# A graph layer on one core: four groups' last two tiles fetched row by row on SP's queue, with four smaller edits

## The chip, the cores and the metric

The kernel runs on one core of one Trainium2 chip. The metric is the device time of one execution in microseconds (us). Before the change the median of 3 runs is 2490.05 us (2479.22 to 2493.46).

## The reference

There are 12500 nodes with 64 features, and 200000 edges sorted by their destination, each with a source, a destination and 32 features of its own. Everything is float32.

```python
msg_in = concatenate([nodes[row], nodes[col], edge_features])      # 64 + 64 + 32
messages = relu(msg_in @ mW1 + mb1) @ mW2 + mb2                    # 160 -> 128 -> 64
aggregated = segment_sum(messages, col)
out = relu(concatenate([nodes, aggregated]) @ uW1 + ub1) @ uW2 + ub2
x = layernorm(x + out)
```

## The kernel before, in words

**Tables.** The first layer of the message network is linear, so it is split: A = x @ mW1[:64] and B = x @ mW1[64:128] + mb1 are computed once for all nodes (`products`, `chunk_a`, `chunk_b`) and stored in DRAM as tables of 128 numbers a row. An edge then needs a row of A (by source), a row of B (by destination) and its own features times mW1[128:].

**Tiles and groups.** 128 edges are a tile (1563 of them). Six tiles are a group s (261), two groups a supergroup g (131). The main loop runs over groups; each of the five engines has its instructions in one order, which is written by hand as the order of the calls in the loop. It is this order that decides what waits for what.

**One group.** SP loads windows of B (`windows`, L282 or L284: 32 consecutive rows of B serve one or several tiles, since edges are sorted by destination; the position comes from a register that L276 loads). SP also loads the destinations, broadcast over partitions, into the operand `l` (`loadd`, L233); DVE turns them into a one-hot selection by comparing with each partition's node number, which L243 prepares (`select`, L243, L245, L251); then SP loads the edge features into the other partitions of the same operand (`load`, L264), behind L245. PE multiplies `l` with the windows (`edge_part`, L374), which gives the B part and the edge part of all six tiles in PSUM (`pc`).

The A part comes in one of two ways. POOL gathers the rows of A of a tile by an indirect transfer, one for each tile (`gather`, L217), up to ten groups ahead into nine row buffers. Or, in 104 of the groups (the list `COPIED`, spaced by the rates in `PACE`), the last two tiles are not gathered: ACT and DVE copy the columns of x of the 2 x 128 source nodes out of a copy of x that lies in SBUF, one pair of columns in an instruction (`singly` on ACT, L345; `joined` on DVE, L352; their addresses are loaded into registers in L322), and PE multiplies them by the weights into `pc` (L377). These copies are spread over the iterations before the group that needs them.

`node_part` adds the gathered rows to `pc` on DVE and applies the relu on ACT (L401 and L402 for whole groups; L397, L398 and L399 for copied ones). `collect` sums h by destination with PE (L434), and counts edges (L431) for the bias term. Every eight groups or so a stretch of nodes is complete: `close` moves the sums and the counts from PSUM to SBUF (L448 and L449, both on ACT), `carry` takes the last 32 nodes over into the next stretch, and `update` to `store` compute and write the result (L471 to L525).

**How many windows.** One window serves 12 tiles at first and fewer as the loop goes on, since later edges lie sparser: 6 from group 32 on, 4 from 64, 3 from 98, 2 from 130, and one for every tile from group 196 on. SP's transfers for a group grow accordingly from one or less to six.

Of the kernel before, what the change touches and what calls it, by code (L numbers as in the profile page):

```python
# [24 lines left out]
SUB = 6  # L25
SUP = 12
NSUP = -(-NT // SUP)
NTP = NSUP * SUP
EPAD = NTP * P
NSUB = -(-NT // SUB)  # L30
WIN = 32
# [15 lines left out]
UW = UN + WIN  # L47
# [22 lines left out]
XBASE = 8320  # L70
U8 = mybir.dt.uint8
YBASE = XBASE + 4 * XCOLS
LEAD = 8
PACE = ((11, 0.413), (50, 0.44), (130, 0.424), (261, 0))
FINAL = 258


# [5 lines left out]
COPIED = []  # L83
for s in range(NSUB):
    while progress(s) >= len(COPIED) + 1 and s + 3 < FINAL:
        COPIED.append(s + 3)
LAST = 4 * (N - 1)
ACTS, CHUNK = 64, 8

# [14 lines left out]

UPD = updates()

UL = min(UB * P, -(-int(N * (1 - (UPD[-1] * SUB * P / E) ** 2) + WIN // 2) // 64) * 64)


@with_exitstack  # L110
def gnn_kernel(ctx: ExitStack, tc: tile.TileContext, x1T, x, eT, e_rows, src, src_row, dst, dst_row, wlist, wrow, wnext, whalf,
# [24 lines left out]
    nc = tc.nc  # L136
# [4 lines left out]
    A = dram.tile([NPAD, DH], F32, name="tab_a")  # L141
# [11 lines left out]
    col_a = const.tile([P, 2, P, 2], I32, name="col_a")  # L153
# [4 lines left out]
    xw = [const.tile([P, UB * P], F32, name=f"xw{k}") for k in range(2)]  # L158
# [17 lines left out]
    pidx = const.tile([P, 1], F32, name="pidx")  # L176
# [1 line left out]
    zero_b = const.tile([P, UW], BF, name="zero_b")  # L178

    cpool = ctx.enter_context(tc.tile_pool(name="cpsum", bufs=1, space=bass.MemoryType.PSUM))  # L180
    cps = cpool.tile([P, WIN + SUP], F32, name="cps")
    slot = cps[:, :WIN]
    drc = const.tile([P, NT], F32, name="drc")
    flag_i = const.tile([1, 1], I32, name="flag_i")
# [3 lines left out]
    wh = const.tile([P, NTP // 2], I32, name="wh")  # L188
# [11 lines left out]
    def tiles(s):  # L200
        return range(s * SUB, min((s + 1) * SUB, NT))

    def gathered_tiles(s):
        return tiles(s)[:SUB - 2 * (s in COPIED)]

    def gather(s):

# [14 lines left out]
    with tc.tile_pool(name="sup", bufs=2) as sup, tc.tile_pool(name="work", bufs=2) as work, tc.manual_schedule():  # L222
# [3 lines left out]
        def loadd(g):  # L226
# [6 lines left out]
                nc.sync.dma_start(l[q:q + WIN].bitcast(I32), dv[:, b].broadcast_to([WIN, SUP // 2, P]))  # L233
            L[g] = l

        def select(g, at=None):


            nt = min(SUP, NT - g * SUP)
            l = L[g]  # L240
            c = WIN + SUP // 2 * (g % 2)
            node = cps[:, c:c + SUP // 2]
            nc.vector.tensor_scalar(node, wh[:, g * SUP // 2:(g + 1) * SUP // 2], pidx, None, op0=ALU.add)  # L243
            for r in ([slice(0, P)] if g > 2 else [slice(q, q + WIN) for q in SK]):
                nc.vector.tensor_tensor(l[r], l[r].bitcast(I32),  # L245
                                        node[r].unsqueeze(2).broadcast_to([r.stop - r.start, SUP // 2, P]),
                                        op=ALU.is_equal)
            if at is not None:
                joined(at, 1, 3)
            s = sup.tile([P, SUP, WIN], F32, name="sel")  # L250
            nc.vector.tensor_tensor(s[:, :nt], slot.unsqueeze(1).broadcast_to([P, nt, WIN]),  # L251
                                    drc[:, g * SUP:g * SUP + nt].unsqueeze(2).broadcast_to([P, nt, WIN]),
                                    op=ALU.is_equal)
            S[g] = s
# [92 lines left out]
        def joined(s, part, of):  # L347

            todo = [(o, k, ACTS + e) for o, k, lo, hi in portion(s, P - ACTS) for e in range(lo, hi, 2)]
            for o, k, a, m in share(todo, part, of):  # L350
                for e, top, bot in addresses(k, a, m, ET.DVE):
                    nc.vector.tensor_tensor(o[:, e:e + 1].bitcast(I32), top.bitcast(I32), bot.bitcast(I32),  # L352
                                            op=ALU.bitwise_or)

        xc = {}

        def parts(n):

            if n == SUB:
                return [(slice(0, 2), SUB // 2)]  # L360
            return [(slice(b, b + 1), (n - b + 1) // 2) for b in range(2) if n > b]
# [18 lines left out]
        def node_part(s):  # L380

            n = len(tiles(s))
            pc = pcs.pop(s)
            h = work.tile([P, 2, SUB // 2, DH], F32, name="h")
            if s < XG:
                xt = xs.pop(s)
                for i in range(n):
                    k, b = divmod(i, 2)
                    q = 64 * b
                    nc.tensor.matmul(pc[:, b, k, :], xt[q:q + 64, k, :], w1a[q:q + 64], start=False,  # L390
                                     stop=i + 2 >= n)
                nc.scalar.activation(h, pc, AF.Relu)
            else:
                a = xg.pop(s)[0].rearrange("p (b k) f -> p b k f", b=2)
                if s in COPIED:
                    m = SUB // 2 - 1
                    nc.vector.tensor_tensor(h[:, :, :m], pc[:, :, :m], a[:, :, :m], op=ALU.add)  # L397
                    nc.scalar.activation(h[:, :, :m], h[:, :, :m], AF.Relu)  # L398
                    nc.scalar.activation(h[:, :, m:], pc[:, :, m:], AF.Relu)  # L399
                for b, m in parts(n) if s not in COPIED else []:  # L400
                    nc.vector.tensor_tensor(h[:, b, :m], pc[:, b, :m], a[:, b, :m], op=ALU.add)  # L401
                    nc.scalar.activation(h[:, b, :m], h[:, b, :m], AF.Relu)  # L402
            hs[s] = h
# [41 lines left out]
        def close(u):  # L445

            ps, pn = sums.pop(u)
            nc.scalar.copy(xw[u % 2][0:1, :UW], pn)  # L448
            nc.scalar.copy(sums_s[u % 2], ps)  # L449

        us = {}
# [117 lines left out]
        def zeros(i, n):  # L569

            w = XCOLS // n
            for t in (xtop[D:], xbot[:D]):
                nc.scalar.activation(t[:, i * w:(i + 1) * w], ident[:D, 0:1].broadcast_to([D, w]), AF.Copy, scale=0.0)
# [80 lines left out]
        for k, c in enumerate(range(0, NB, NCH)):  # L654
            chunk_a(c)
            if k == 0:
                chunk_b(0, [B0v, Bv])
            if k == 2:

                w0 = wint[:, :GE * SUP // SUB * LS]  # L660
                nc.vector.tensor_scalar(past, w0[:, GE * SUP // SUB * LS - 1:], float(EARLY - WIN), None, op0=ALU.is_gt)
                nc.vector.tensor_scalar(w0, w0, float(EARLY - WIN), None, op0=ALU.min)
                windows(0)
                windows(1)
            if k == 4:
                relative(0, 8 * SUP)
            if k == 6:
                offsets()
            if k == 9:
                select(0)  # L670
                load(0)
                counts(0)

        def rest(s):

            if 3 <= s < 9 and s % 2:
                others((s - 3) // 2 * 4, (s - 3) // 2 * 4 + 4)
            if 3 <= s < 11:
                zeros(s - 3, 8)
            if s == 9:  # L680
                columns_list()
            if s == 1:
                relative(8 * SUP, 8 * SUP + WCH)
            elif s == 2:
                relative(8 * SUP + WCH, NT)
                halves(4 * SUP, NTP // 2)
            elif s == BS:
                nc.sync.dma_start(wa, wrow.rearrange("o (p c) -> (o p) c", c=NSUP))
                nc.sync.dma_start(wb, wnext.rearrange("o (p c) -> (o p) c", c=NSUP))
# [12 lines left out]
            elif s == BS + 2:  # L702
                weights()
                checks()
# [49 lines left out]
        n = UPD[K - 1]  # L754
# [8 lines left out]
        for s in range(last + 2):  # L763
            g, j = divmod(s, SUP // SUB)
# [54 lines left out]
            if s == UPD[K - 1]:  # L819
                columns(K - 1)  # L820
            rest(s)
            joined(s, 2 if j == 0 and g + 1 < NSUP else 1, 3 if j == 0 and g + 1 < NSUP else 2)
            singly(s, 0, 1)
            if s in due and due[s] + 2 < K:
# [5 lines left out]
            if earlier(5) is not None:  # L830
# [4 lines left out]
                          skip_runtime_bounds_check_because="a count of edges")  # L835
    with tc.If(flag > 0), tc.tile_pool(name="gen", bufs=1) as up:
# [25 lines left out]
        first = up.tile([P, 1], F32, name="first")  # L862
        nc.vector.tensor_scalar(first, spare, -1.0, float(NPAD + P), op0=ALU.mult, op1=ALU.add)

        with tc.For_i(0, NT, 1) as t:
# [26 lines left out]
            pc = psum.tile([P, DH], F32, name="pcg", tag="pc")  # L892
# [4 lines left out]
            h = up.tile([P, DH], F32, name="hg")  # L897
# [104 lines left out]
```

## Time and profile before

| | us |
|---|---|
| median of 3 runs | 2490.05 |
| the profiled execution, in all | 2486.88 |
| its span, first to last instruction | 2485.1 |
| PE, ACT, POOL, DVE busy | 1630.3, 1612.1, 1280.4, 1118.3 |
| mean granted TensorE clock | 0.535 of full speed |

Busy time of an engine doesn't count the instructions of its sequencer: register loads, address arithmetic, semaphores and the issuing of transfers. SP does nothing else, so it has no busy share at all, and is read from the waits of its queue ("SPq") and from the timeline. "issue" is time in which an engine waited for nothing that the profile shows. In a row of waits stand the engine and the line, what was waited for, the time in all, how often, and the longest.

### The profile page before, as it was taken

The numbers are of one execution on the slowest core, as the hardware profiler recorded it, in microseconds if no ns is written. First come the engines' busy times: TensorE is split into PE (matmuls) and PEld (weight loads), VectorE is DVE, ScalarE is ACT, GpSimd is POOL, SyncE is SP. The second block draws the span as 40 slices with busy tenths as digits, with TensorE's granted clock in tenths as the row PEclk, the third lists the DMA queues.
The fourth block names the chain that finished last, engine by engine and source line by source line (L and its number), as shares of the span: only waits on it lengthen the run. The fifth ranks groups of instructions, "written<-read, shape, count | busy, mean of one in ns | idle before, by whom it ended". The sixth has DMA issues, their size and how long they took to land. (4 is left out here: it accounts for less than half of the span.)

```text
span 2485.1 us, 47640 instructions
## 1 busy us (share of the span) xinstructions
PE 1630.3 (66%) x9652; PEld 1392.7 (56%) x9652; DVE 1118.3 (45%) x7843; ACT 1612.1 (65%) x7232; POOL 1280.4 (52%) x1364
## 2 busy tenths in 40 slices
PE   1238575666566666666567666776667777777878
PEld 1237465655555555555555555555556656666666
DVE  0211554544444544445444444544544444544544
ACT  0015676767777767768776766776767776777754
POOL 7153455555555555545555555555555555555540
PEclk7565555555555555555555555555555555555556
DMA  5343232322222222222222222222222222222222
GB/s 131 104 120 84 71 91 78 89 78 71 69 67 65 74 64 72 68 68 72 71 71 75 76 69 74 78 75 76 74 75 73 75 78 79 76 77 74 80 72 53
DMA packets 207229, 191.63 MB, mean 77 GB/s; under 512 B 57243, under 2 KB 173297, under 8 KB 206945
## 3 DMA queue, kind: packets, MB, share of 16 engines
q0 software_dynamic: 43360, 86.92, 13.7%
q1 hardware_dynamic: 149040, 92.72, 13.5%
q10 hardware_dynamic: 14546, 8.93, 1.3%
q8 instruction: 91, 1.49, 0.3%
q14 instruction: 192, 1.57, 0.2%
HBM read 170.65 MB, written 17.76 MB: 76 GB/s over the span
## 5 line engine op out<-in xcount | busy, mean ns | idle before, releaser
L217 POOL DMA_INDIRECT xg<-tab_a,src_s x1295 | 1222.6, 944 | 1120.5 <-DVE h L401 403.3
L345 ACT ACTIVATE xc<-xtop,xbot 128x1 f32 x6656 | 1302.3, 281 | 296.7 <-issue 274.0
L352 DVE TENSOR_TENSOR xc<-xtop,xbot 128x1 int32 x6656 | 597.0, 154 | 630.8 <-issue 609.9
L434 PE MATMUL sums<-sel,h 128*128 128x32 f32 x3126 | 688.6, 385 | 140.0 <-issue 82.2
L434 PEld LDWEIGHTS sums<-sel,h 128*128 128x128 f32 x3126 | 655.9, 313 | 168.8 <-issue 82.7
L374 PE MATMUL pc<-rhs,l 64*128 64x128 f32 x3126 | 478.1, 436 | 355.3 <-DVE h L401 85.5
L374 PEld LDWEIGHTS pc<-rhs,l 64*128 64x128 f32 x3126 | 392.2, 309 | 431.7 <-issue 169.0
L245 DVE TENSOR_TENSOR l<-l,cps 128x768 f32<-128x768 int32 (+1 forms) x134 | 127.8, 954 | 167.9 <-remote 84.1
L402 ACT ACTIVATE h<-h 128x768 f32<-128x768 f32 (+1 forms) x148 | 122.5, 829 | 115.0 <-DVE h L401 100.1
L431 PEld LDWEIGHTS <-one 128*1 128x1 bf16 x1563 | 66.1, 83 | 225.0 <-issue 213.4
L431 PE MATMUL cnt<-sel,one 128*1 128x32 bf16 x1563 | 113.2, 188 | 112.8 <-issue 111.7
L401 DVE TENSOR_TENSOR h<-pc,xg 128x768 f32<-128x768 f32 (+1 forms) x148 | 140.4, 949 | 89.5 <-remote 30.4
L397 DVE TENSOR_TENSOR h<-pc,xg 128x512 f32<-128x512 f32 x104 | 71.8, 690 | 183.2 <-remote 71.6
L398 ACT ACTIVATE h<-h 128x512 f32<-128x512 f32 x104 | 64.8, 623 | 106.1 <-DVE h L397 83.4
L251 DVE TENSOR_TENSOR sel<-cps,drc 128x384 f32<-128x384 f32 x131 | 72.0, 549 | 102.0 <-PE sums L434 75.8
L377 PE MATMUL pc<-w1a,xc 64*128 64x128 f32 x416 | 82.9, 398 | 2.0 <-issue 2.0
L590 ACT COPY tb<-pb 128x512 f32<-128x512 f32 (+1 forms) x13 | 7.4, 569 | 114.6 <-remote 74.7
L580 PE MATMUL pb<-w1a,xtop 64*128 64x128 f32 x100 | 25.1, 435 | 84.8 <-DVE tb L588 59.5
L377 PEld LDWEIGHTS pc<-w1a,xc 64*128 64x128 f32 x416 | 73.8, 313 | 2.5 <-issue 2.5
L471 PE MATMUL pu<-xw,uz 128*128 128x448 f32 (+1 forms) x68 | 61.2, 1000 | 18.0 <-DVE h L401 12.4
L493 ACT COPY y<-py 128x256 f32<-128x256 f32 x33 | 12.0, 364 | 93.9 <-remote 67.8
L580 PEld LDWEIGHTS pb<-w1a,xtop 64*128 64x128 f32 x100 | 22.3, 325 | 87.2 <-DVE tb L588 61.3
(104 smaller groups left out, 965.7 us busy)
## 6 DMA issues: line engine op xcount, KB each, us to landing
l<-in_dst_row SPq DMA_DIRECT2D x262, 96.0 KB
l<-in_eT SPq DMA_DIRECT2D x262, 96.0 KB
xg<-tab_a,src_s POOLq DMA_INDIRECT x1295
rhs<-tab_b SPq DMA_DIRECT2D x361, 32.0 KB
tab_b<-tb SPq DMA_DIRECT2D x13, 512.0 KB
rhs<-tab_b SPq DMA_DIRECT2D x387, 16.0 KB
tab_a<-tb ACTq DMA_DIRECT2D x12, 512.0 KB
out<-y SPq DMA_DIRECT2D x33, 128.0 KB
```

What stands on the lines that cost most here:

```text
L217: nc.gpsimd.indirect_dma_start(out=a[:, i, :] if s < XG else a[:, i // 2, i % 2, :], out_offset=None, in_=A[:, :] if s >= XG else x[:, :], ...
L245: nc.vector.tensor_tensor(l[r], l[r].bitcast(I32), node[r].unsqueeze(2).broadcast_to([r.stop - r.start, SUP // 2, P]), op=ALU.is_equal)
L251: nc.vector.tensor_tensor(s[:, :nt], slot.unsqueeze(1).broadcast_to([P, nt, WIN]), drc[:, g * SUP:g * SUP + nt].unsqueeze(2).broadcast_to( ...
L345: nc.scalar.activation(o[:, e:e + 1], top.bitcast(F32), AF.Identity, bias=bot.bitcast(F32))
L352: nc.vector.tensor_tensor(o[:, e:e + 1].bitcast(I32), top.bitcast(I32), bot.bitcast(I32), op=ALU.bitwise_or)
L374: nc.tensor.matmul(pc[:, b, k, :], L[g][q:q + 64, m, :], rhs[g % 2][q:q + 64, w, :], start=s >= XG or k == 0, stop=s >= XG and not copied)
L377: nc.tensor.matmul(pc[:, b, k, :], xc[s][q:q + 64], w1a[q:q + 64], start=False, stop=True)
L397: nc.vector.tensor_tensor(h[:, :, :m], pc[:, :, :m], a[:, :, :m], op=ALU.add)
L401: nc.vector.tensor_tensor(h[:, b, :m], pc[:, b, :m], a[:, b, :m], op=ALU.add)
L402: nc.scalar.activation(h[:, b, :m], h[:, b, :m], AF.Relu)
L431: nc.tensor.matmul(pn[:, bass.ds(ws[i], WIN)], one, SB[g][:, k0 + i, :, 1], start=False, stop=ends and i == n - 1)
L434: nc.tensor.matmul(ps[:, bass.ds(ws[i], WIN)], h[:, i % 2, i // 2, :], S[g][:, k0 + i, :], start=False, stop=ends and i == n - 1)
```

## The change

Five things change.

1. Four further groups (the list `SINGLE`) are not gathered whole: as in the copied groups, POOL gathers four tiles of six. The rows of A of the other two tiles come by single transfers from table A, one for each edge: one partition, 512 bytes. SP issues them in `fetched`, called once an iteration near its end, for as many edges as `ROWPACE` allows (3.5 an iteration from group 12, 3.0 from 45, 2.3 from 90, 1.6 from 136, in even numbers), two transfers an edge; one register load brings the addresses of a portion. DVE adds the gathered part and the fetched part in two instructions.
2. `close` copies the counts on DVE, not on ACT.
3. The node numbers that L243 computed for each supergroup are computed in three long instructions (`first_nodes`) and kept in PSUM, 80 supergroups at a time.
4. In a copied group DVE adds into PSUM, in place, and ACT applies one relu to all six tiles.
5. `PACE` is raised by about 1.5%, so that 105 groups are copied.

```diff
-PACE = ((11, 0.413), (50, 0.44), (130, 0.424), (261, 0))
+PACE = ((11, 0.42), (50, 0.446), (130, 0.429), (261, 0))
...
+ROWPACE = ((12, 3.5), (45, 3.0), (90, 2.3), (136, 1.6))
+SINGLE, QUOTA = [], {}
+step, found = ROWPACE[0][0], 0.0
+while step < NSUB - 8:
+    done, a = 0, step
+    while done < P and step < NSUB - 8:
+        found += next(r for b, r in reversed(ROWPACE) if step >= b)
+        n = min(int(found) // 2 * 2, P - done)
+        found -= n
+        QUOTA[step] = len(SINGLE), done, done + n
+        done += n
+        step += 1
...
+    SINGLE.append(next(c for c in range(step + 1, NSUB) if c not in COPIED))
+    step = SINGLE[-1] + 1
...
+NODES = 80
...
-    cps = cpool.tile([P, WIN + SUP], F32, name="cps")
+    cps = cpool.tile([P, WIN + NODES * SUP // 2], F32, name="cps")
...
-        return tiles(s)[:SUB - 2 * (s in COPIED)]
+        return tiles(s)[:SUB - 2 * (s in COPIED or s in SINGLE)]
...
+        def first_nodes(a, b):
+            c = WIN + SUP // 2 * (a % NODES)
+            nc.vector.tensor_scalar(cps[:, c:c + SUP // 2 * (b - a)], wh[:, SUP // 2 * a:SUP // 2 * b], pidx, None, op0=ALU.add)
...
-            c = WIN + SUP // 2 * (g % 2)
+            c = WIN + SUP // 2 * (g % NODES)
             node = cps[:, c:c + SUP // 2]
-            nc.vector.tensor_scalar(node, wh[:, g * SUP // 2:(g + 1) * SUP // 2], pidx, None, op0=ALU.add)
...
+        def fetched(s):
+            if s not in QUOTA or QUOTA[s][1] == QUOTA[s][2]:
+                return
+            i, lo, hi = QUOTA[s]
+            k = SINGLE[i] - LEAD
+            if lo == 0:
+                xr[SINGLE[i]] = work.tile([P, 2, DH], F32, name="xr", bufs=1)
+            o = xr[SINGLE[i]]
+            _, v = nc.values_load_multi_w_load_instructions(
+                col_a[k % P:k % P + 1, k // P].rearrange("k e b -> k (e b)")[:, 2 * lo:2 * hi], engines=[ET.SP], min_val=XBASE,
+                max_val=YBASE + LAST, skip_runtime_bounds_check_because="sources are node numbers")
+            for e in range(lo, hi):
+                for b, first in enumerate((XBASE, YBASE)):
+                    w = v[2 * (e - lo) + b].with_bounds(min_val=first, max_val=first + LAST, guaranteed_mod_val=0, out_of_modulus=4)
+                    nc.sync.dma_start(o[e:e + 1, b], A4[bass.ds(w - first, 4), :].rearrange("c d -> (c d)").unsqueeze(0))
...
                 if s in COPIED:
                     m = SUB // 2 - 1
+                    nc.vector.tensor_tensor(pc[:, :, :m], pc[:, :, :m], a[:, :, :m], op=ALU.add)
+                    nc.scalar.activation(h, pc, AF.Relu)
+                if s in SINGLE:
+                    m = SUB // 2 - 1
                     nc.vector.tensor_tensor(h[:, :, :m], pc[:, :, :m], a[:, :, :m], op=ALU.add)
-                    nc.scalar.activation(h[:, :, :m], h[:, :, :m], AF.Relu)
-                    nc.scalar.activation(h[:, :, m:], pc[:, :, m:], AF.Relu)
+                    nc.vector.tensor_tensor(h[:, :, m], pc[:, :, m], xr[s], op=ALU.add)
+                    nc.scalar.activation(h, h, AF.Relu)
...
-            nc.scalar.copy(xw[u % 2][0:1, :UW], pn)
+            nc.vector.tensor_copy(xw[u % 2][0:1, :UW], pn)
...
+                first_nodes(0, 8)
                 select(0)
...
+            if s == 6:
+                first_nodes(8, NODES)
+            if s == 2 * NODES - 3:
+                first_nodes(NODES, NSUP)
...
             rest(s)
+            fetched(s)
             joined(s, 2 if j == 0 and g + 1 < NSUP else 1, 3 if j == 0 and g + 1 < NSUP else 2)
```

More of the change, by code (lines that the diff above doesn't have):

```diff
@@ L86 @@
         COPIED.append(s + 3)
+ROWPACE = ((12, 3.5), (45, 3.0), (90, 2.3), (136, 1.6))
[10 more added lines that the diff above has]
+        step += 1
+    if done < P:
+        QUOTA = {k: v for k, v in QUOTA.items() if k < a}
+        break
+    SINGLE.append(next(c for c in range(step + 1, NSUB) if c not in COPIED))
+    step = SINGLE[-1] + 1
 LAST = 4 * (N - 1)
@@ L355, in gnn_kernel @@
         xc = {}
+        A4 = A.rearrange("n (c d) -> (n c) d", c=4)
+        def fetched(s):
[13 more added lines that the diff above has]
+                    nc.sync.dma_start(o[e:e + 1, b], A4[bass.ds(w - first, 4), :].rearrange("c d -> (c d)").unsqueeze(0))
+        xr = {}
         def parts(n):
@@ L396, in node_part @@
                     m = SUB // 2 - 1
+                    nc.vector.tensor_tensor(pc[:, :, :m], pc[:, :, :m], a[:, :, :m], op=ALU.add)
+                    nc.scalar.activation(h, pc, AF.Relu)
+                if s in SINGLE:
+                    m = SUB // 2 - 1
                     nc.vector.tensor_tensor(h[:, :, :m], pc[:, :, :m], a[:, :, :m], op=ALU.add)
-                    nc.scalar.activation(h[:, :, :m], h[:, :, :m], AF.Relu)
-                    nc.scalar.activation(h[:, :, m:], pc[:, :, m:], AF.Relu)
-                for b, m in parts(n) if s not in COPIED else []:
+                    nc.vector.tensor_tensor(h[:, :, m], pc[:, :, m], xr[s], op=ALU.add)
+                    nc.scalar.activation(h, h, AF.Relu)
+                for b, m in parts(n) if s not in COPIED and s not in SINGLE else []:
                     nc.vector.tensor_tensor(h[:, b, :m], pc[:, b, :m], a[:, b, :m], op=ALU.add)
```

## The prediction

> **What bounds the kernel now.** I read the page from above: engines, then who waits for whom, then SP's own queue by stage, because the change puts over a thousand transfers on that queue.
>
> ```profile
> PE 1630.3 (66%) x9652; PEld 1392.7 (56%) x9652; DVE 1118.3 (45%) x7843; ACT 1612.1 (65%) x7232; POOL 1280.4 (52%) x1364
> L217 POOL DMA_INDIRECT xg<-tab_a,src_s x1295 | 1222.6, 944 | 1120.5 <-DVE h L401 403.3 <-issue 352.0 <-DVE h L397 248.9
> L345 ACT ACTIVATE xc<-xtop,xbot 128x1 f32 x6656 | 1302.3, 281 | 296.7 <-issue 274.0 <-DMA ub_s<-in_ub 17.0
> L352 DVE TENSOR_TENSOR xc<-xtop,xbot 128x1 int32 x6656 | 597.0, 154 | 630.8 <-issue 609.9 <-DMA xg<-tab_a,src_s 4.3
> ```
>
> No engine is full. POOL, whose gathers the change relieves, waits 403 + 249 us for DVE to free a row buffer: it is not the limit, so a gather saved isn't time saved. SP has no busy share on the page, and its queue has to be asked by itself. The next rows are the largest wait of SP's queue in five stretches: 248:545, 545:945, 945:1358, 1358:1905 and 2000:2400 us (of the last also the second).
>
> ```profile
> SPq L264 <- DVE l L245: 103.4, 11, 22.8
> SPq L264 <- DVE l L245: 146.9, 17, 15.4
> SPq L264 <- DVE l L245: 114.3, 15, 15.0
> SPq L264 <- DVE l L245: 44.8, 17, 7.1
> SPq L282 <- remote: 3.8, 9, 1.5
> SPq L282 <- PE pc L374: 2.4, 7, 0.4
> ```
>
> While SP waits for DVE's comparison L245 it is ahead of the rest; that is its spare time. It shrinks stage by stage and is gone in the last one (about 14 us of 400, all rows together). There SP is the one that is late, as the waits of the other engines in 2000:2400 say:
>
> ```profile
> PE pc L374 <- DMA l<-in_eT: 43.0, 14, 6.6
> DVE l L245 <- DMA l<-in_dst_row: 39.7, 15, 5.6
> PE pc L374 <- DMA rhs<-tab_b: 10.3, 10, 2.1
> ```
>
> All three transfers are SP's. The chain that ended last, asked for 2403:2412, runs through SP too, in steps of 0.7 us for one instruction:
>
> ```profile
> 2405.36 0.72 issue
> 2406.09 0.70 SPq L282
> ...
> 2406.80 0.72 issue
> 2407.53 0.73 SPq L282
> ```
>
> The timeline of SP shows both of its speeds (start, length, how many transfers are merged; POOL's rows tell when gathers ran, and the last row is of the view by line):
>
> ```profile
> 2006.16 1.95 SPq L282 DMA_DIRECT2D rhs<-tab_b  x4
> 2010.70 7.28 SPq L282 DMA_DIRECT2D rhs<-tab_b  x6
> 17.90 0.30 SPq L647 DMA_DIRECT2D wint<-in_wlist  x1
> 2007.86 0.94 POOL L217 DMA_INDIRECT xg<-tab_a,src_s  x1 [3.11 <-DVE h L397]
> 2010.36 0.94 POOL L217 DMA_INDIRECT xg<-tab_a,src_s  x1 [0.30 <-issue]
> L282 SPq DMA_DIRECT2D rhs<-tab_b x263: 3/316/896, 2001.8 to 2399.6; - x132
> ```
>
> Undisturbed, one transfer with an address from a register takes (1.95 - 0.32) / 3 = 0.54 us from start to start; disturbed, 7.28 / 6 = 1.2 us.
>
> **The change, part by part.** From the constants in the diff I worked out that 105 groups instead of 104 are copied, the four single groups are 51, 97, 161 and 243, and their 4 x 128 x 2 = 1024 row transfers are issued in 204 portions, one register load each. Placed in the trace by the group that is running (one add L401 or L397 on DVE for each from group 10 on):
>
> - groups 12 to 44 (248:545): 228 transfers, 33 loads
> - 45 to 89 (545:945): 260, 43
> - 90 to 135 (945:1358): 200, 44
> - 136 to 195 (1358:1905): 188, 47
> - 196 to 241 (1905:2313): 148, 37
>
> **The row transfers on SP.** A single row of 512 B isn't in this trace. Its instructions are those of L282 (address arithmetic, semaphore, move, transfer). One contiguous run, `wint`, took SP 0.30 us as a transfer, against the 0.316 of L282's 32 rows, so the small size buys little; a row comes cheaper than 0.54 us only if its transfer is. Floor: 0.54 us. Dear end: what SP paid on average where it was never idle, 2000:2400, with these issues and this load:
>
> ```profile
> rhs<-tab_b SPq DMA_DIRECT2D x263, 16.0 KB
> l<-in_eT SPq DMA_DIRECT2D x44, 96.0 KB
> l<-in_dst_row SPq DMA_DIRECT2D x42, 96.0 KB
> out<-y SPq DMA_DIRECT2D x10, 128.0 KB
> xw<-in_x1T SPq DMA_DIRECT2D x10, 113.8 KB
> L276 SPq TENSOR_LOAD <-wint x245: 4/711/1392, 90.6 to 2461.4; - x123
> ```
>
> That is 369 transfers and about 44 loads of 0.71 us in 400 - 14 us: (386 - 31) / 369 = 0.96 us a transfer. With both prices (loads at 0.71), against the wait shown above:
>
> - first: 123 + 23 = 146 us (dear 242), wait 103: over by 43 (139)
> - second: 140 + 31 = 171 (281), wait 147: over by 24 (134)
> - third: 108 + 31 = 139 (223), wait 114: over by 25 (109)
> - fourth: 102 + 33 = 135 (213), wait 45: over by 90 (168)
> - fifth: 80 + 26 = 106 (168), wait 0: over by 106 (168)
>
> Over by 288 us at the floor, 718 at the dear price. Below the floor nothing is excluded: rows could be nearly free, which gives 0. In the first three stages 92 us of floor cost are left, and SP has smaller waits there that I haven't counted, so I put these at nothing and keep the 92 for the range. The last two stages have no cover, and I take them at the floor, 90 + 106 = 196 us. Why the floor: a stage that is stretched by SP has the same gathers in it, and the slow steps of SP lie beside gathers (in the rows above POOL was idle for 3.11 us before 2007.86, when four transfers took 1.95 us, and gathering at 2010.36, when six took 7.28); the time added is then time without gathers. Queued behind the rows on SP, and so late next, are the windows of B, the edge loads L264 and the destination loads L233, in other words PE's L374 and DVE's L245.
>
> The Trainium skill ("DMA: Bandwidth & Descriptors", section "Anatomy of one DMA — SWDGE (gpsimd) path") puts the sequencer's dispatch of a transfer at some 50 ns; for all 1024 that would be an estimated 51 us, and SP would hide them in its waits. The trace disagrees for SP: 0.54 us undisturbed. The same page's "Rules for kernel authors" speaks against the change: transfers under 64 KB pay mostly overhead; the rows above of 16 KB agree.
>
> **POOL.** Ten gathers fewer (8 of the single groups, 2 of one more copied group). Between gathers stand 0.30 us of issue (the row at 2010.36), so 10 x (0.944 + 0.30) = 12.4 us less, on an engine that waits 650.
>
> **ACT and DVE.**
>
> ```profile
> L399 ACT ACTIVATE h<-pc 128x256 f32<-128x256 f32 x104 | 38.0, 366 | 1.8 <-issue 1.4
> L398 ACT ACTIVATE h<-h 128x512 f32<-128x512 f32 x104 | 64.8, 623 | 106.1 <-DVE h L397 83.4 <-remote 13.4 <-issue 9.2
> L392 ACT ACTIVATE h<-pc 128x768 f32<-128x768 f32 x10 | 8.0, 803 | 24.9 <-remote 13.6 <-PE pc L390 4.6 <-PE sums L434 4.0
> L448 ACT COPY xw<-cnt 1x480 f32<-1x480 f32 x34 | 18.2, 534 | 18.9 <-remote 18.3 <-PE cnt L431 0.5
> L251 DVE TENSOR_TENSOR sel<-cps,drc 128x384 f32<-128x384 f32 x131 | 72.0, 549 | 102.0 <-PE sums L434 75.8 <-remote 15.9 <-PE pc L377 5.9
> L401 DVE TENSOR_TENSOR h<-pc,xg 128x768 f32<-128x768 f32 (+1 forms) x148 | 140.4, 949 | 89.5 <-remote 30.4 <-PE pc L374 18.5 <-PE sums L434 13.2
> L243 DVE TENSOR_SCALAR cps<-wh,pidx 128x6 f32<-128x6 int32 x131 | 28.8, 220 | 6.9 <-issue 6.8
> L588 DVE COPY tb<-pb 128x512 f32<-128x512 f32 x12 | 8.3, 689 | 64.5 <-ACT tb L590 58.8 <-issue 5.7
> L397 DVE TENSOR_TENSOR h<-pc,xg 128x512 f32<-128x512 f32 x104 | 71.8, 690 | 183.2 <-remote 71.6 <-PE pc L374 45.2 <-issue 39.8
> ```
>
> One relu of 768 from PSUM (L392's form) for two: 38.0 + 64.8 - 105 x 0.803 = 18.5 us less on ACT. The add in PSUM isn't in the trace; L397 reads PSUM already and I leave it at 690 ns, bounds 0.55 (the 384-element comparison) to 0.95 us (the 768-element add), that is -15 to +27 us in all on DVE. Counts: 18.2 us off ACT, and at up to 0.69 us (L588, 512 elements) 34 x 0.69 = 23 us onto DVE. First nodes: 28.8 us off DVE, three long ones of 48, 432 and 306 elements put back some 2 us. One more copied group: 64 more copies, 64 x (1302.3 + 274.0) / 6656 = 15 us on ACT and 64 x (597 + 610) / 6656 = 12 us on DVE, and four matmuls on PE. A single group's second add of 256 elements costs DVE about what the shorter first one saves. ACT: 18.5 + 18.2 - 15 = 22 us less; DVE: 23 + 2 + 12 - 29 = 8 us more. Where SP sets the pace, ACT's relief only lengthens ACT's wait, so I count 0; where rows are hidden it counts half to all, 11 to 22 us.
>
> Sum: 2486.9 us (the profiled execution, span 2485.1) + 196 = 2683; the median of the runs is 3 us above that execution, so 2685.
>
> **The rivals.**
>
> **The rows are hidden; faster.** SP's order has slack for them and ACT's 22 us and POOL's 12 come through in part: 2487 - 20 = 2467. For it: SP's waits of 103 to 147 us in the first three stages nearly hold the rows at the floor price, and the fast row of four in 1.95 us. Against it: the last two stages. It decides if a row transfer costs under (45 - 33) / 188 = 0.06 us in the fourth stage, or if SP's 0.7 us steps turn out to be waiting for others rather than SP's own pace. The skill's 50 ns would give this result.
>
> **SP keeps its dear price.** The slow steps go with SP's work and not with the gathers: 2487 + 718, some 3200. For it: 0.96 us is the mean of 369 transfers. Against it: the fast stretches whenever POOL pauses.
>
> **Rows hidden, but DVE in the way.** The copy of the counts stands on DVE ahead of the selection and waits there for PE, as ACT did (18.9 us before L448), and everything in DVE's order waits with it: the 8 us above and 19 of waiting, 2487 + 27, some 2514. Against it: the counts come first in PE's work on a group, and DVE has idle time of its own.
>
> **How the numbers follow.** Forecast, SP overruns at a price between the floor of the last two stages and a little over all five (2600 to 2880): 0.56. Dear price, above 2900: 0.11. DVE in the way, 2500 to 2560: 0.07. Hidden and faster, 2440 to 2477: 0.21. No change: 0.05. The runs of before lie 14 us apart (0.57%), so 0.5% is about what can be told from no change. Faster 0.21, same 0.05, slower 0.74. The range goes from 2465, which cuts the hidden case in half, to 2900: it leaves out about 0.1 below and 0.1 above. The likeliest case alone is 2600 to 2880.
>
> **What would show it.** In the profile after, transfers xr from tab_a, 1024 of them, on SP's queue; SP's wait for L245 gone or nearly gone in all five stages; PE's waits for in_eT and rhs and DVE's for in_dst_row grown from 93 us in 400 to several times that, and now in the early stages as well; POOL's share under 50% with longer waits for DVE's h; the stretch from group 136 to 241 about 200 us longer, the first three stages little changed. On ACT L448 gone and one relu of about 0.8 us for a copied group; on DVE L243 gone. If SP still waits for DVE in groups 136 to 241, the central step is wrong and the price of a row was far under 0.54 us. If the first stages stretch by over 100 us each, the dear price was right.

## The result, and the profile after

The changed kernel takes 2619.13 us (2611.86 to 2630.02, 4 runs) against 2487.25 (2479.22 to 2493.46, 4 runs) on the same chip: the ratio is 1.0536, with an interval of 1.0481 to 1.0591, or 132 us more. The profiled execution took 2612.94 us (span 2611.1), at a mean granted clock of 0.551.

First the page of the changed kernel: busy time by engine, one of the costliest groups, and the new transfers.

```profile
PE 1667.9 (64%) x9656; PEld 1421.6 (54%) x9656; DVE 1108.1 (42%) x7817; ACT 1586.0 (61%) x7158; POOL 1274.3 (49%) x1354
L268 DVE TENSOR_TENSOR l<-l,cps 128x768 f32<-128x768 int32 (+1 forms) x134 | 127.6, 952 | 331.7 <-DMA l<-in_dst_row 241.1
xr<-tab_a SPq DMA_DIRECT2D x1024, 0.5 KB
```

The same comparison of DVE before, from the view by line:

```profile
L245 DVE TENSOR_TENSOR l<-l,cps 128x768 f32<-128x768 int32 (+1 forms) x134 | 127.8, 954 | 167.9 <-remote 84.1 <-DMA l<-in_dst_row 51.5 <-issue 25.4
```

ACT is busy 26 us less than before, DVE 10, POOL 6, and PE 38 us more; no engine comes nearer to being full. DVE's comparison (now L268) waits 241 us in all for the destinations that SP brings, after 52. The 1024 row transfers are on SP's queue. They are half a MB of the 192 MB that the transfers move in all, and on the pages the busiest hardware queue takes 13.0% of the DMA engines' time after 13.5%: it is not the DMA engines that became short.

SP's largest wait in each of the five stages (253:558, 558:978, 978:1403, 1403:1977 and 1977:2456 us) answers to the five rows of before:

```profile
SPq L287 <- DVE l L268: 12.0, 1, 12.0
SPq L287 <- DVE l L268: 9.8, 1, 9.8
SPq L307 <- PE pc L417: 2.3, 4, 0.7
SPq L307 <- PE pc L417: 4.3, 10, 0.6
SPq L305 <- PE pc L417: 2.2, 8, 0.4
```

SP waited 103, 147, 114 and 45 us for DVE in the first four stages; now it never waits to speak of, from the first row transfer to the last. The others wait for SP instead. These are the waits of DVE and PE for SP's transfers in 1977:2456, and then two of them in 558:978:

```profile
DVE l L268 <- DMA l<-in_dst_row: 107.3, 21, 9.0
PE pc L417 <- DMA l<-in_eT: 70.1, 16, 7.6
PE pc L417 <- DMA rhs<-tab_b: 17.3, 17, 2.2
...
PE pc L417 <- DMA l<-in_eT: 43.3, 8, 9.9
DVE l L268 <- DMA l<-in_dst_row: 20.1, 9, 3.9
```

In the last stage they are 195 us of 479, after 93 of 400 before.

Where the time came from, by the first add of each group on DVE (the first group's start of one stage to that of the next):

```
groups      before    after   difference
 12 to 44    296.7    305.4     +8.7
 45 to 89    400.3    419.9    +19.6
 90 to 135   412.6    425.3    +12.7
136 to 195   547.1    573.8    +26.7
196 to 231   326.9    374.4    +47.5
232 to 241    95.3    105.1     +9.8
242 to 257   132.2    129.6     -2.6
```

The two profiled executions lie 126 us apart. Of these, 57 lie in groups 196 to 241, 27 in 136 to 195 and 41 in the three stages before. SP's own time answers for them. I added up the time from the start of each instruction on SP to the start of the next, by line (us, before to after, in three of the stages):

```
                               45 to 89         136 to 195       196 to 231
row transfers (L396)             0 to 227         0 to 172         0 to 98
their register loads (L390)      0 to 30          0 to 26          0 to 15
edge loads with their wait     224 to 36        110 to 34         17 to 16
windows of B                   107 to 70        325 to 232       250 to 180
one such row transfer               0.88             0.91             0.85
one window, the commonest     1.81 to 1.18     1.84 to 1.28     1.17 to 0.83
slow steps of some 0.7 us       95 to 174       205 to 246       166 to 154
```

(Slow steps are those within 50 ns of 0.71 us or of two or three times it, whatever the instruction. Their sum hangs on this limit: all steps over 0.6 us but waits at semaphores come to 117 to 261, 316 to 360 and 169 to 179.) A row transfer costs 0.85 to 0.91 us on average, dear; but the windows between them became cheaper by a third. In the last stage 98 + 15 us came and 70 went, which leaves most of the 47.5. The source view of L396 and the timeline of SP show both speeds:

```profile
L396 SPq FUSED_REGOPS  x1024: 3/46/1154, 257.8 to 2463.5; - x171
L396 SPq DMA_DIRECT2D xr<-tab_a x1024: 3/228/1397, 258.0 to 2463.7; - x171
```

```profile
2103.18 6.32 SPq L305 DMA_DIRECT2D rhs<-tab_b  x6
2109.52 1.40 SPq L252 DMA_DIRECT2D l<-in_dst_row  x2
2111.09 3.10 SPq L305 DMA_DIRECT2D rhs<-tab_b  x6
2114.30 0.82 SPq L287 DMA_DIRECT2D l<-in_eT  x2
2115.89 1.56 SPq L396 DMA_DIRECT2D xr<-tab_a  x4
```

Six windows take 6.32 us or 3.10, and four rows undisturbed (1.56 - 0.23) / 3 = 0.44 us each from start to start, of which the transfer instruction is 0.228 (its median in the source view). The rows stand on SP between the edge load of one group and the windows of the next, so those start later.

POOL's gathers and the small edits, in the view by line:

```profile
L236 POOL DMA_INDIRECT xg<-tab_a,src_s x1285 | 1216.4, 947 | 1251.8 <-DVE h L448 498.4 <-issue 339.1 <-DVE pc L440 302.8
L441 ACT ACTIVATE h<-pc 128x768 f32<-128x768 f32 x105 | 85.0, 809 | 286.8 <-DVE pc L440 278.5 <-remote 5.1 <-issue 1.8
L440 DVE TENSOR_TENSOR pc<-pc,xg 128x512 f32<-128x512 f32 x105 | 73.4, 699 | 238.1 <-remote 93.8 <-PE pc L420 46.4 <-PE sums L481 37.4
L495 DVE COPY xw<-cnt 1x480 f32<-1x480 f32 x34 | 21.5, 634 | 1.2 <-PE cnt L478 1.2
L258 DVE TENSOR_SCALAR cps<-wh,pidx 128x48 f32<-128x48 int32 (+2 forms) x3 | 1.4, 479 | 0.0
```

The add in PSUM takes 699 ns after 690, the one relu 809 ns, the counts 634 ns on DVE after 534 on ACT. The counts hardly wait there (1.2 us in all). The first nodes have shrunk from 28.8 us to 1.4.

### The profile page after: what moved, and what is told of

It is laid out like the page before. It is cut to its first block, busy times and chain, and to the rows that moved or that the text cites. A ratio compares the mean times of both kernels' runs of the same rounds, so it can differ in the third digit from the quotient of the medians.

```text
span 2611.1 us, 50795 instructions
## 1 busy us (share of the span) xinstructions
PE 1667.9 (64%) x9656; PEld 1421.6 (54%) x9656; DVE 1108.1 (42%) x7817; ACT 1586.0 (61%) x7158; POOL 1274.3 (49%) x1354
## 5 line engine op out<-in xcount | busy, mean ns | idle before, releaser
L236 POOL DMA_INDIRECT xg<-tab_a,src_s x1285 | 1216.4, 947 | 1251.8 <-DVE h L448 498.4
L368 ACT ACTIVATE xc<-xtop,xbot 128x1 f32 x6720 | 1289.3, 280 | 140.1 <-issue 118.0
L417 PE MATMUL pc<-rhs,l 64*128 64x128 f32 x3126 | 518.9, 445 | 701.6 <-issue 328.8
L417 PEld LDWEIGHTS pc<-rhs,l 64*128 64x128 f32 x3126 | 415.8, 311 | 799.9 <-issue 672.3
L375 DVE TENSOR_TENSOR xc<-xtop,xbot 128x1 int32 x6720 | 587.9, 154 | 502.0 <-issue 483.9
L481 PE MATMUL sums<-sel,h 128*128 128x32 f32 x3126 | 696.2, 391 | 61.3 <-issue 25.9
L268 DVE TENSOR_TENSOR l<-l,cps 128x768 f32<-128x768 int32 (+1 forms) x134 | 127.6, 952 | 331.7 <-DMA l<-in_dst_row 241.1
L441 ACT ACTIVATE h<-pc 128x768 f32<-128x768 f32 x105 | 85.0, 809 | 286.8 <-DVE pc L440 278.5
L448 DVE TENSOR_TENSOR h<-pc,xg 128x768 f32<-128x768 f32 (+1 forms) x143 | 135.6, 949 | 174.6 <-PE pc L417 112.1
L440 DVE TENSOR_TENSOR pc<-pc,xg 128x512 f32<-128x512 f32 x105 | 73.4, 699 | 238.1 <-remote 93.8
L478 PE MATMUL cnt<-sel,one 128*1 128x32 bf16 x1563 | 101.0, 189 | 10.2 <-issue 9.7
L236 POOL DMA_INDIRECT xg<-in_x,src_s x60 | 56.9, 949 | 19.2 <-issue 18.0
L532 PE MATMUL py<-ux,xw 128*128 128x64 f32 x268 | 64.2, 418 | 2.2 <-DVE h L448 2.2
```

Source lines behind the costliest of these rows:

```text
L236: nc.gpsimd.indirect_dma_start(out=a[:, i, :] if s < XG else a[:, i // 2, i % 2, :], out_offset=None, in_=A[:, :] if s >= XG else x[:, :], ...
L268: nc.vector.tensor_tensor(l[r], l[r].bitcast(I32), node[r].unsqueeze(2).broadcast_to([r.stop - r.start, SUP // 2, P]), op=ALU.is_equal)
L368: nc.scalar.activation(o[:, e:e + 1], top.bitcast(F32), AF.Identity, bias=bot.bitcast(F32))
L417: nc.tensor.matmul(pc[:, b, k, :], L[g][q:q + 64, m, :], rhs[g % 2][q:q + 64, w, :], start=s >= XG or k == 0, stop=s >= XG and not copied)
L478: nc.tensor.matmul(pn[:, bass.ds(ws[i], WIN)], one, SB[g][:, k0 + i, :, 1], start=False, stop=ends and i == n - 1)
L481: nc.tensor.matmul(ps[:, bass.ds(ws[i], WIN)], h[:, i % 2, i // 2, :], S[g][:, k0 + i, :], start=False, stop=ends and i == n - 1)
```

## The experiments

**Theory SP:** the row transfers use up SP's spare time and then push back its windows, destinations and edge loads; the other edits are small gains. **Rival DVE:** the copies of counts, the add in PSUM and DVE's order cost the time. **Rival price:** the slow steps belong to SP's work, so each row costs what SP paid on average, wherever it is put. One thing is needed to read the numbers: the program of before takes about 2480 to 2487 us on some chips and about 1716 on others, so each run below is compared with the kernel before on its own chip.

**The small edits alone** (changed kernel, no row transfers):

```diff
+SINGLE, QUOTA = [], {}
 LAST = 4 * (N - 1)
```

> The changed kernel without its row transfers: no single groups, the four small edits kept (105 copied groups, one relu and the add in PSUM, counts on DVE, node numbers kept in PSUM). Theory SP (the row transfers make SP late): the loss is gone, 2465 to 2490 us, and SP waits for DVE's comparison about as long as before (103, 147, 114, 45 us in the first four stages). Rival DVE (the small edits put DVE in the way): 2600 us or more, DVE's waits stay as in the changed kernel.

Measured 2457.74 us against 2479.77: ratio 0.992 (0.9896 to 0.9944), 22 us less. The time lies 7 us under the range expected. SP waits for DVE's comparison again, in the stages 243:545, 545:939, 939:1349 and 1349:1885 of this kernel:

```profile
SPq L288 <- DVE l L269: 71.2, 8, 23.2
SPq L288 <- DVE l L269: 121.0, 17, 10.8
SPq L288 <- DVE l L269: 74.4, 13, 11.8
SPq L288 <- DVE l L269: 45.2, 15, 7.4
```

These are somewhat shorter than before (103, 147, 114 and 45 us); another 30, 50, 54 and 16 us of the same line's waits stand there under "remote", an origin that the profile can't name.

The same kernel on another chip of the slower kind:

> The changed kernel without the row transfers, once more, for a chip on which the kernel before takes 1716 us. There ACT is busy 90% of the span, so the 22 us taken off ACT and the 12 off POOL should come through: theory SP 1690 to 1712 us, against 1873 with the rows. Rival, the small edits share in the loss there: 1740 or more. On a chip with 2480 for the kernel before: 2450 to 2470 as the first time.

Measured 2455.44 against 2486.34: ratio 0.9888 (0.9853 to 0.9923). The small edits are a gain of about 1% on this kind of chip (on the faster kind they were not measured), so the rival DVE is out. The row transfers cost what the changed kernel loses and what the small edits gain, each against the kernel before on its own chip: 132 + 22, some 154 us.

**The row transfers alone** (kernel before with `SINGLE`, `QUOTA`, `fetched` and the two adds of a single group, none of the other edits):

```diff
+ROWPACE = ((12, 3.5), (45, 3.0), (90, 2.3), (136, 1.6))
...
+            fetched(s)
             joined(s, 2 if j == 0 and g + 1 < NSUP else 1, 3 if j == 0 and g + 1 < NSUP else 2)
```

> The kernel before with the row transfers alone (four single groups, none of the small edits, 104 copied groups). Theory SP: 2610 to 2645 us, the changed kernel's time plus what the small edits save there, 0 to 22 us. Rival DVE: 2475 to 2500 us.

Measured 2637.2 against 2479.77: ratio 1.0653 (1.0613 to 1.0694), 157 us more. The changed kernel loses 132 against the kernel before on its chip, so beside the rows the small edits bring some 25 us (18 between the two medians as they are). Alone they brought 22 and 31: the two parts add up.

**Three single groups of four** (the one whose rows go out in groups 162 to 241 is left out):

```diff
+SINGLE = SINGLE[:3]
+QUOTA = {k: v for k, v in QUOTA.items() if v[0] < 3}
```

> The changed kernel with the first three single groups alone; no row is fetched after group 158. Theory SP: what the rows cost follows SP's spare time, so the fourth group is the dearest: groups 196 to 241, which took 57 us longer than before, are back at the time of before, and groups 162 to 195 give back some 15 more: 2540 to 2555 us. Rival, the same price for every row: a quarter of the loss goes, 2588 us.

Measured 2521.99 against 2479.77: ratio 1.0157 (1.0121 to 1.0194). Groups 196 to 231 take 331.9 us and 232 to 241 take 89.7, as without any rows (330.8 and 89.5). The three groups cost 2522 - 2458 = 64 us on this chip. The fourth alone cost the rest of the changed kernel's loss, 132 - 42 = 90 us with each run against its own chip's kernel before (97 between the two medians). Both expectations were too high.

**One group, slowly and early** (256 row transfers, one edge for every group from 12 to 139):

```diff
-ROWPACE = ((12, 3.5), (45, 3.0), (90, 2.3), (136, 1.6))
+ROWPACE = ((12, 1.0),)
...
+SINGLE = SINGLE[:1]
+QUOTA = {k: v for k, v in QUOTA.items() if v[0] < 1}
```

> The changed kernel with one single group whose 256 row transfers are spread over groups 12 to 139 (two edges, four transfers, every second iteration; some 2 us of SP for a group at the measured 0.87 us a transfer, against 3 us of wait). Theory SP: hidden, the time of the run without rows within 10 us. Rival, the same price for every row (126 us / 1024): 31 us above the run without rows.

Measured 2460.56 against 2479.77: ratio 0.9932 (0.9906 to 0.9957), within 3 us of the kernel without rows. In 245:1338, where all but a few of its rows go out, SP still waits:

```profile
SPq L289 <- DVE l L270: 111.6, 26, 20.3
SPq L289 <- remote: 102.2, 12, 14.7
```

256 row transfers cost next to nothing where SP has this spare time; the rival price, by which a row costs the same wherever it is put, is out. By the same sum from start to start a row took SP 0.95 us on average here: a dear price paid out of SP's waits doesn't appear in the kernel's time. Whether the slow steps belong to SP's work or to the gathers, this run doesn't tell. Nor do the rows bring anything: the two gathers that they save on POOL show in no time saved.

**One group, late** (the same number of rows, in groups 162 to 241):

```diff
+SINGLE = SINGLE[3:]
+QUOTA = {k: (0, *v[1:]) for k, v in QUOTA.items() if v[0] == 3}
```

> The changed kernel with the fourth single group alone: 256 row transfers in groups 162 to 241, as many as in the run with one group slowly, at another place. Theory SP: no spare time there, so they cost what those groups lost in the changed kernel, 57 us from group 196 on and some 15 before: 2515 to 2535 us. Rival, place doesn't matter: 2460 us.

This ran on a chip of the faster kind: 1803.42 against 1715.73, ratio 1.051 (1.0481 to 1.054), 88 us more. The stages up to group 135 are unchanged there; 136 to 195 takes 397 us after 374, 196 to 231 takes 281.5 after 230, 232 to 241 takes 79.4 after 65. (The stages compared with are those of the kernel with one relu, below, on the same chip.) The same number of transfers cost 3 us early and 88 late. Those two runs were on chips of different kinds, and so the expected 2515 to 2535 can't be compared; but the 90 us above are for the same late group on the slower kind.

**The change as it is, on a chip of the faster kind:**

> The changed kernel once more, since the last four runs were on a chip on which the kernel before takes 1716 us instead of 2480. Theory SP, where the kernel before takes about 1716: a row costs SP 0.45 us there (the run with one late group) and its waits are 113, 140, 100, 75 and 20 us in the five stages, so the rows are over by 8 + 1 + 14 + 36 + 67 = 126 us: 1830 to 1865 us. Where it takes about 2480: 2610 to 2630 as before. Rival, the loss belongs to the slow chip: below 1760 on the other.

Measured 1873.03 against 1715.24: ratio 1.0915 (1.0892 to 1.0938), 158 us more, some 8 us above the upper end expected. The source view of the rows, and two waits in 1376:1738, groups 196 to 241:

```profile
L396 SPq FUSED_REGOPS  x1024: 46/46/61, 135.7 to 1744.2; - x171
L396 SPq DMA_DIRECT2D xr<-tab_a x1024: 220/228/838, 135.9 to 1744.4; - x171
...
DVE l L268 <- DMA l<-in_dst_row: 62.9, 21, 5.0
PE pc L417 <- DMA l<-in_eT: 25.4, 13, 4.7
```

The address arithmetic of a row takes 46 to 61 ns here, against up to 1154 on the slower kind, and a row 0.45 us on average from start to start, against 0.87: SP runs undisturbed nearly always, and the change costs even more. On this kind of chip it is the number of SP's instructions that costs the time, not the slow steps.

**No gathers for 21 groups** (kernel before without the gathers of groups 205 to 225; tests whether the slow steps belong to the gathers):

```diff
+BARE = range(205, 226)
...
+        if s in BARE:
+            xg[s] = xtop[:, :SUB * DH], None
+            return
```

> The kernel before, with the gathers of groups 205 to 225 left out (their A part is replaced by numbers that lie in SBUF, so the output is not the reference's). Theory, the gathers slow SP: in these groups SP's steps of 0.7 us are gone, a window transfer takes 0.55 us instead of 1.2, SP waits for DVE again, and the groups run at some 7.5 us instead of 9.0: 2450 to 2465 us. Rival, SP's pace is its own (its transfers or its instructions): SP's steps stay, the period stays near 9.0: 2475 to 2490 us.

This ran on a chip of the faster kind, where SP has few slow steps anyway: 1710.61 against 1715.73, ratio 0.9968 (0.9954 to 0.9982). By itself it says nothing on the question. The same kernel on the slower kind:

> The run without gathers in groups 205 to 225 (the output is not the reference's), once more, for a chip on which the kernel before takes 2480 us. Theory, the gathers slow SP: no steps of 0.7 us on SP in these groups, 0.55 us a window transfer, period 7.5 us instead of 9.0: 2440 to 2460. Rival, SP's steps don't depend on gathers: 2470 to 2490. On a chip with 1716 us: 1705 to 1712 as the first time.

Measured 2415.86 against 2486.34: ratio 0.9712 (0.9662 to 0.9763), 70 us less, more than expected. Groups 196 to 231 take 267.8 us after 326.9. The source view of the single windows in 1995:2100, where no gather runs, and the timeline of SP in it:

```profile
L286 SPq FUSED_REGOPS  x102: 37/37/42, 1997.1 to 2098.9; - x102
L286 SPq MOVE rhs<-tab_b x102: 29/29/29, 1997.2 to 2099.0; - x102
L286 SPq DMA_DIRECT2D rhs<-tab_b x102: 315/316/1141, 1997.3 to 2099.1; - x102
```

```profile
2051.64 3.63 SPq L286 DMA_DIRECT2D rhs<-tab_b  x6
2058.34 3.10 SPq L286 DMA_DIRECT2D rhs<-tab_b  x6
```

Against the same view of before in 2000:2400, where gathers run:

```profile
L282 SPq FUSED_REGOPS  x263: 3/37/729, 2000.8 to 2399.1; - x132
L282 SPq MOVE rhs<-tab_b x263: 3/29/1423, 2001.1 to 2399.6; - x132
```

The address arithmetic takes 37 to 42 ns without gathers and up to 729 ns with them, the move 29 and up to 1423. The longest transfers are no shorter (1141 ns, and 896 with gathers), so it is the small instructions that go faster. A window costs SP 0.60 us instead of 1.17, by the limit above a single slow step of 0.7 us is left in 120 us (register loads still take 0.77 to 1.1 us), and SP waits for DVE again (1990:2110):

```profile
SPq L268 <- DVE l L249: 8.4, 8, 3.0
```

Slow steps, on this kind of chip, go with gathers. How much of the 70 us is SP's speed and how much the gathers that are missing this run can't part; that the same edit brought 5 us on the faster kind, where gathers leave SP undisturbed, speaks for SP's speed, but the two kinds differ in more than that.

**Half of the single windows** (kernel before, every second one of the single windows is not loaded; a direct relief of SP in the last stage):

```diff
                 k, b = divmod(t % SUP, 2) if n == 1 else (t % SUP // n, 0)
+                if n == 1 and b:
+                    continue
```

> The kernel before, with every second window transfer left out from group 196 on (old numbers stay in their place, so the output is not the reference's): SP has three transfers less for a group there, about 3.5 us of its 9. Theory, SP bounds the last stage of the kernel before: PE's waits for in_eT and rhs and DVE's for in_dst_row (93 us in 400) go, and the 62 groups run 0.5 to 1.0 us faster each: 2420 to 2455 us. Rival, SP only looks busy and the other engines set the pace as they do at 9.1 us in the stage before: 2475 to 2490 us.

> The run with every second window transfer left out from group 196 on (the output is not the reference's), once more, for a chip on which the kernel before takes 2480 us. Theory, SP bounds the last stage of the kernel before on that chip: 0.5 to 1.0 us less for each of 62 groups, 2420 to 2455 us. Rival: 2470 to 2490 us. On a chip with 1716 us for the kernel before, as the first time: within 0.3% of it, since SP still waits for DVE there.

Both times the chip was of the faster kind: 1714.91 against 1715.73 (0.9992, 0.9981 to 1.0003) and 1714.84 against 1715.24 (0.9996, 0.9986 to 1.0006). There SP doesn't set the pace of the last stage in the kernel before, and still becomes the bound once the rows are added. On the slower kind this was not measured, so that SP alone sets the pace of that stage in the kernel before is borne out by its waits only.

**One relu alone** (kernel before with the add in PSUM and one relu for a copied group):

```diff
-                    nc.vector.tensor_tensor(h[:, :, :m], pc[:, :, :m], a[:, :, :m], op=ALU.add)
-                    nc.scalar.activation(h[:, :, :m], h[:, :, :m], AF.Relu)
-                    nc.scalar.activation(h[:, :, m:], pc[:, :, m:], AF.Relu)
+                    nc.vector.tensor_tensor(pc[:, :, :m], pc[:, :, :m], a[:, :, :m], op=ALU.add)
+                    nc.scalar.activation(h, pc, AF.Relu)
```

> The kernel before with the add in PSUM and one relu in the copied groups alone. By the sum of the prediction ACT has 18.5 us less to do (38.0 + 64.8 - 104 x 0.803), of which half to all comes through: 9 to 19 us faster, 2461 to 2471 against 2480. Rival, the add in PSUM is dear on DVE (up to 27 us more): no gain or slower.

On a chip of the faster kind: 1713.35 against 1715.73, ratio 0.9987 (0.9976 to 0.9998), 2.4 us less; the 9 to 19 us expected were for the slower kind, where this edit was not measured alone. Its page and two rows of SP's waits (130:1291, then groups 196 to 241 in 1290:1585):

```profile
PE 1484.2 (87%) x9652; PEld 1280.2 (75%) x9652; DVE 1097.0 (64%) x7843; ACT 1541.4 (90%) x7128; POOL 1282.1 (75%) x1364
...
SPq L264 <- DVE l L245: 424.3, 92, 19.3
SPq L264 <- DVE l L245: 21.4, 14, 3.5
```

ACT is 90% busy there, and yet the 18.5 us that the prediction's sum takes off its work are worth 2.4. So busy time saved on ACT isn't always time saved, and the 22 us of all the small edits on the slower kind can't be put down to one edit of them. On the faster kind SP waits 424 us for this comparison up to group 195, and 21 after it.

## Why the prediction was right, and where its sizes were off

**Right: direction and mechanism, and in part the place.** 2619 lies in the forecast case (2600 to 2880), 66 us under the 2685. SP's waits are gone in all five stages. The transfers queued behind the rows are late: destinations for DVE, edge loads and windows for PE. The waits for them doubled in the last stage, though, where several times as much was expected. POOL's share is 49%, and its waits for DVE's buffers grew from 652 us to 801 (498.4 for L448 and 302.8 for L440). The kernel without rows and the one with rows only show the two parts apart, and the one late group shows the place.

**Too high: the floor price of a row in the last two stages.** The sum put 106 us into groups 196 to 241 and 90 into 136 to 195; they grew by 57 and 27 (by 59 and 38 against the kernel without rows, which leaves out the small edits' gain). The prediction's bounds for the last stage, 1905:2313, end some 14 us early: group 242 starts at 2327. A row takes 0.44 us undisturbed, not 0.54. Its transfer instruction is 228 ns and not the 316 of 32 rows: the prediction judged by the `wint` transfer of 0.30 us that the small size buys little, and that was the wrong row to judge by. A row also has no semaphore instruction of its own (17 ns in a window), which the prediction counted in. A register load took 15.2 us for the 116 transfers of groups 196 to 231, in 29 portions, so 0.52 us each and not 0.71. That gives 148 x 0.44 + 37 x 0.52 = 84 us. The other 27 are time that SP had lost before and lost no longer. By line, in groups 196 to 241, the rows and their loads took 140 us, the windows' own loads 6 more, and the windows 89 less, which makes 57. SP's waits gave 8 us of the 27: all rows of its waits together fell from 16 us to 8. (The prediction read about 14 in 400; those rows add up to 12.5.) The rest should be slow steps, but their sum in these groups went from 216 to 193 us by the limit above and from 216 to 232 by the wider one, so this last part isn't shown.

**Right by its reason: why the floor and not the dear price.** The prediction said that slow steps go with the gathers, so that added work is paid at the undisturbed price. The mean price of a row was in fact dear, 0.85 to 0.91 us, near the 0.96 of the dear end. But the slow steps that fell on the rows were taken from the windows, 1.17 to 0.83 us each, and their sum stayed nearly the same where SP was never idle before (166 to 154 us, or 169 to 179 by the wider limit). That price could have been read as proof of the dear case by anyone who looked at the rows alone. The run without gathers shows the tie between slow steps and gathers directly, on this kind of chip.

**Wrong: nothing in the first three stages.** They grew by 8.7, 19.6 and 12.7 us, 41 together; the floor's sums had 43, 24 and 25, and these were set aside with the remark that SP has smaller waits that were not counted. Such waits are there (in groups 45 to 89 the edge loads gave up 188 us and not 147), but the rows were paid at 0.88 there: slow steps grew from 95 to 174 us, probably because SP now works beside gathers during which it had waited. The errors of the early stages and of the last two have opposite signs, and the total is nearer than its parts; that much of its closeness is luck.

**ACT and DVE.** The prediction worked out 22 us less on ACT and counted none of it where SP sets the pace, and up to all of it where rows are hidden. Without rows the kernel gains 22 and 31 us, and one group hidden early gains 19; and with all rows the small edits still bring 18 to 25, so "0 where SP sets the pace" was too low by that. The single durations held: 699 ns for the add in PSUM (690 taken), 634 for the counts (up to 690), 809 for the relu (803). The rival of DVE in the way has no room: the counts wait 1.2 us in all.

**POOL.** The prediction said that a gather saved isn't time saved, since POOL waits. The run with one early group bears that out for two gathers. But leaving out the 108 gathers of 21 groups brought 70 us on this kind of chip, an estimated 0.65 us each: where SP sets the pace, a gather can cost time through SP. Ten gathers would be some 6 us by this, too few to be seen beside the rows.

**On the hidden case.** It was given 0.21 with the condition of under 0.06 us for a row. The Trainium skill's 50 ns for a sequencer's dispatch ("DMA: Bandwidth & Descriptors", section "Anatomy of one DMA — SWDGE (gpsimd) path"), which it gives for transfers issued by GpSimd, spoke for it; on SP the transfer instruction alone is 228 ns, and a row takes 0.44 us with its address arithmetic and move. The same page of the Trainium skill, section "Issuing engines are not separate DMA queues", says that the sequencer's time to start a transfer is usually small beside the transfer itself. Small or not beside one transfer, which no row here shows, it is SP's time for 1024 of them, 0.44 us and more each, that used up SP's waits and made the rest late.

**Which kernel is best.** The changed kernel without its row transfers, at 2457.74 against 2479.77 and 2455.44 against 2486.34, beats both on the slower kind of chip; on the faster kind it was not measured. One group fetched early is as good and no better.

## What to carry to other kernels

A queue that issues transfers has no busy row, so ask how long it waits in each stage: that wait is the budget for what one wants to add, and where it is zero each added instruction delays all that stands behind it. Put added transfers where the wait is, or leave them out. A saving on an engine that waits anyway, as POOL does here, may be worth nothing, as with the two gathers of the early group; it is worth something only through what it slows, as with the gathers of 21 groups. And when the price of an added instruction is measured, look at what its neighbours on the queue cost before and after: a mean price can hold time that was only moved.

## What the runs showed of the hardware that was not expected

- The same program of before takes 2480 to 2487 us (medians) on some chips and about 1716 on two others, with a mean granted clock of 0.53 to 0.55 there and about 0.58 here. On the faster kind SP's slow steps are nearly absent: beside gathers the address arithmetic of a row takes 46 to 61 ns. What makes the chips differ stays open.
- On the slower kind, SP's small instructions take up to some 0.7 us or a multiple while gathers run: the address arithmetic up to 729 ns against 37 to 42 without gathers. Why is open.
- A row transfer of 512 B takes SP 228 ns against 316 for 32 rows of 512 B; both cost their address besides, and come to 0.44 and 0.54 us from start to start.
